# One more step between a chunk's norm and its transposes, and layer 0's last pieces in another order

## The chip, the cores and the metric

The kernel runs on one core of one Trainium2 chip. The metric is the time of one execution on the device, in microseconds (us); lower is better. Times of a kernel are the median of several runs. The profile that is read here comes from one more execution, with the hardware profiler on; its own time stands in the table below.

## What is computed

Two layers work on two images of 128 channels and 64 by 64 points. Layer 0 is a neighbourhood attention block (7 by 7 windows, 4 heads, norms and three linear maps). Layer 1 is a full self-attention over the 4096 tokens of an image, followed by a causal convolution with 16 spectral filters. Cut to what matters for this change:

```python
t = _to_tokens(x)                       # (2, 4096, 128)
t = t + _L1_attn_ref(_ln_t(t))          # softmax(q q^T / sqrt(128), diagonal masked) q
t = t + _L1_ffn_ref(_ln_t(t), ...)      # spectral filters and three short lags
```

The second norm, `_ln_t(t)` after the attention, is the "chunk's norm" of the title. The kernel takes it for 512 tokens at a time, as soon as these 512 tokens have all their attention.

## The kernel before

Layer 0 is written as small pieces (functions named like `t3.pw` or `k.z`), which a table of due times, `PLAN`, sorts. There are 16 bands of 512 tokens, numbered 0 to 15; `t.yr[12]` below is the piece `t.yr` of band 12. Pieces that start with `k` prepare layer 1 for image 0: `k.a` transposes 512 tokens of image 0, `k.tt` copies them, `k.bn` and `k.pw` take the norm's statistics (`k.pw` on POOL), `k.z` applies the norm on POOL in four instructions (L704), `k.b` transposes the normed tokens back on PE (L193), and `k.cm` copies them (L716). Most pieces are issued in a row (`now`, L844). The rest goes into two lists: `chunk_` holds the seven `k` pieces of the last band (15), `later` holds 65 `t` pieces of bands 12 to 15. Before the change they are simply joined (L841). They are issued by `drain` (L1209), three pieces and then a `yield`.

Layer 1's attention (`attention`, L881) treats an image as 8 chunks of 512 tokens and walks over the 36 pairs of chunks `(a, c)` with `a <= c`. For each of the four 128-token tiles of a pair it issues on PE: the scores of the next pair (L898, "weights", one 128x512 product; ACT then takes the exponential, L905), the product with the values (L951 `other`, or L926 `own` where `a == c`), and a product with a turned tile that is left from before (L926 with `et`). After two tiles of a pair with `a != c` come eight 128x128 transposes (L912), whose result DVE copies and sums (L915, tile `et`). After each of the four tiles the code calls `fill()`: this is a slot, into which one step of other work goes.

`filler` (L1189) decides which. It has two queues of generators: `urgent`, for the work that follows a chunk's attention, and `steps`, for work with no hurry (`drain`, the branch weights, the filters' transforms, the tokens of image 1; in the second attention what is left of the first, the mixing of the filter matrices, the loading of blocks). A slot takes one step of `urgent`, and of `steps` only if `urgent` is empty. When row `a` of pairs is finished, `after(b, c, part)` (L968) joins `urgent`. Its steps, with a `yield` after each:

1. PE transposes the chunk's result (L975), DVE divides by the softmax sums and adds the residual (L980).
2. The norm: on DVE `bn_stats` and `bn_aggr` (L174, L175), an add (L164), on POOL a power (L165), on DVE four multiply-subtracts into the tile `z` (L182).
3. PE transposes `z` (L193, four instructions), ACT copies the result into `zc` (L991).
4. and 5. PE multiplies `z` with the transform matrices (L1010), two products each; copies `ub` on DVE and ACT (L1012), stores of `us` by DMA (SP's queue).
6. The last part of the transform (L1020, L1026, L1028).

There are 16 such chunks. After chunks 4 and 8 of an image, `short_lags` (L1034) joins, with transposes of `tt` (L193) and products with `zc` (L1051). At the end of the second attention, the steps that are left of `after` and `short_lags` are issued alternately with those of a `short_lags` that was kept back (`kept`, L1266 to L1271). Then follows the convolution (from L1283), whose inputs `ut` are read back from `us` (L1295).

In the convolution the order on PE is that of the code (`manual_schedule`), and for layer 0's `now` that of all engines. For the slots of the attention a scheduler may still move neighbouring instructions of one engine past each other when the program is built.

Of the kernel before, what the change touches and what calls it, by code (L numbers as in the profile page):

```python
# [95 lines left out]
def kernel(  # L96
# [89 lines left out]
    def layernorm(dst, src):  # L186

        ln_apply(dst, src, ln_statistics(src))

    def transposed(ps, src):  # L190

        for j in range(src.shape[1]):
            nc.tensor.transpose(ps[:, j * P : (j + 1) * P], src[:, j, :], ident)  # L193
# [30 lines left out]
    with l0a:  # L224
# [607 lines left out]
        now, later, chunk_ = [], [], []  # L832
        for at, k, name, f in events:
# [4 lines left out]
            else:  # L838
                early = True
            (chunk_ if name[:1] == "k" and k == bands[-1] else now if early else later).append(f)  # L840
        later = [*chunk_, *later]  # L841
        engines = mybir.EngineType
        with tc.manual_schedule(engines={engines.PE, engines.DVE, engines.Activation, engines.Pool}):
            for f in now:  # L844
# [12 lines left out]
    with ap_:  # L857
# [6 lines left out]
        def bank():  # L864
            return ps_m.tile([P, 512], F32, tag="bank", name="bank")
# [102 lines left out]
        def after(b, c, part):  # L968

            n0 = 4 * c  # L970
            ph, f0 = divmod(n0, FB)
            par, h = divmod(ph, 2)
            pt = bank()
            for j in range(4):
                nc.tensor.transpose(pt[:, j * P : (j + 1) * P], xa[b][:, (n0 + j) * P : (n0 + j + 1) * P], ident)  # L975
            rden = sp.tile([P, 4], F32, tag="rden", name="rden")
            nc.vector.tensor_reduce(rden, part[:, n0 : n0 + 4, :], AX.X, ALU.add)
            nc.vector.reciprocal(rden, rden)
            for j in range(4):
                nc.vector.scalar_tensor_tensor(  # L980
                    tt[b][:, n0 + j, :], pt[:, j * P : (j + 1) * P], rden[:, j : j + 1], tt[b][:, n0 + j, :],
                    ALU.mult, ALU.add,
                )
            yield
            z = sp.tile([P, 4, P], F32, tag="z4", name="z4")
            layernorm(z, tt[b][:, n0 : n0 + 4, :])
            yield
            pt = bank()
            transposed(pt, z)
            s0 = 1 + h * (TH // 2)  # L990
            nc.scalar.copy(  # L991
                zc[:, par, s0 : s0 + TH // 2].rearrange("p (c f) -> p f c", f=FB)[:, f0 : f0 + 4, :],
                pt.rearrange("p (f c) -> p f c", f=4),
            )
            yield
            z2 = z.rearrange("p f d -> p (f d)")

            def store(m0, q, src):
                nc.sync.dma_start(
                    out=us[m0 // 2 : (m0 + P) // 2, :, 2 * h + q, f0 : f0 + 4, b, par, :].rearrange(  # L1000
                        "g r f d -> (g r) f d"
                    ),
                    in_=src.rearrange("p (f d) -> p f d", d=P),
                )

            for m0 in (0, P):
                for q in range(2):
                    rows_ = slice(q * SB, (q + 1) * SB)
                    pu = bank()
                    nc.tensor.matmul(pu, lhsT=tr[rows_, h, m0 : m0 + P], rhs=z2[rows_], start=True, stop=True)  # L1010
                    ub = sp.tile([P, 512], F32, tag="ub", name="ub", bufs=3)
                    (nc.scalar.copy if q else nc.vector.tensor_copy)(ub, pu)  # L1012
                    store(m0, q, ub)
                yield

            banks = [bank() for q in range(2)]
            for i in range(2):
                for q in range(2):
                    rows_ = slice(q * SB, (q + 1) * SB)
                    nc.tensor.matmul(  # L1020
                        banks[q][i * 64 : (i + 1) * 64, 0:256], lhsT=tr[rows_, h, 2 * P : NC],
                        rhs=z2[rows_, i * 256 : (i + 1) * 256], start=True, stop=True,
                    )
            ub = sp.tile([P, 512], F32, tag="ub", name="ub", bufs=3)
            for q in range(2):
                (nc.scalar.copy if q else nc.vector.tensor_copy)(ub[:, q * 256 : (q + 1) * 256], banks[q][:, 0:256])  # L1026
                for i in range(2):
                    nc.sync.dma_start(  # L1028
                        out=us[P:, :, 2 * h + q, f0 + 2 * i : f0 + 2 * i + 2, b, par, :].rearrange("g r f d -> (g r) f d"),
                        in_=ub[i * 64 : (i + 1) * 64, q * 256 : (q + 1) * 256].rearrange("p (f d) -> p f d", d=P),  # L1030
                    )
            yield

        def short_lags(b, h):  # L1034


            for par in range(2):
                n0 = (par * 2 + h) * FB
                for f0 in range(0, FB, 4):
                    pt = bank()  # L1040
                    transposed(pt, tt[b][:, n0 + f0 : n0 + f0 + 4, :])
                    nc.scalar.copy(xa[b][:, (n0 + f0) * P : (n0 + f0 + 4) * P], pt)
                    yield
                xv = xa[b][:, n0 * P : (n0 + FB) * P].rearrange("p (f c) -> p f c", f=FB)
                for c0 in range(0, P, 64):
                    py = bank()
                    for lag in range(3):
                        from_par = (par - lag) % 2
                        back = (lag - par + from_par) // 2
                        s0 = 1 + (h * P + c0) * FB - back  # L1050
                        nc.tensor.matmul(  # L1051
                            py, lhsT=mu[:, lag, :], rhs=zc[:, from_par, s0 : s0 + 512], start=(lag == 0), stop=(lag == 2)
                        )
                    pv = py.rearrange("p (c f) -> p f c", f=FB)
                    first = h == 0 and c0 == 0
                    for lo, hi, s in ((0, 32, 0), (32, 64, 1)) if first else ((0, 64, 2 + h),):
                        xs = xv[:, :, c0 + lo : c0 + hi]
                        nc.vector.scalar_tensor_tensor(
                            xs, pv[:, :, lo:hi], seg[:, s : s + 1], xs, ALU.mult, ALU.add
                        )  # L1060
                    yield
# [127 lines left out]
        def filler(b, steps, kept=None):  # L1189

            urgent, done = [], []

            def fill(c=None, part=None):
                if c is not None:
                    done.append(c)
                    urgent.append(after(b, c, part))
                    if len(done) % 4 == 0:
                        held = kept if kept is not None and len(done) == 4 else urgent
                        held.append(short_lags(b, len(done) // 4 - 1))
                    return  # L1200
                for queue in (urgent, steps):
                    while queue:
                        if next(queue[0], 0) is None:
                            return
                        queue.pop(0)

            return fill, urgent
# [294 lines left out]
```

## Time and profile before

| what | value |
|---|---|
| median of 3 runs | 2224.06 us (2223.95 to 2224.48) |
| the profiled execution's own time | 2225.03 us |
| its span, first to last instruction | 2223.3 us |
| mean granted TensorE clock | 0.992 |
| layer 0 | up to about 346 us of the span |
| attention of image 0 | about 346 to 829 us |
| attention of image 1 and what is left | about 830 to 1319 us |
| convolution | from 1319.4 us |

How to read the lines that follow further down. A list of waits has the engine and line that waited, the engine and line that ended the wait, then the sum in us, the number of times, and the longest. In a timeline each row is a run of like instructions: start, length, engine, line, operation, result and operands, and in brackets the idle time of the engine just before it and what ended it. `x2` behind a 128x512 product is one product[...]. A table by windows gives the busy time of each engine in a stretch, the mean granted TensorE clock (`PEclk`, 1.00 is full) and the share of the DMA engines.

### The profile page before, as it was taken

What the parts mean: (1) busy time and instruction counts of PE and PEld (TensorE: products, weight loads), DVE (VectorE), ACT (ScalarE), POOL (GpSimd) and SP (SyncE); (2) the same over time, 40 slices, a digit from 0 to 9 for tenths busy, and PEclk for the clock granted to TensorE, in tenths of its full rate; (3) what the DMA queues carried; (4) which work ended last, traced back from release to release, by engine and by line L of the source; (5) the groups of instructions that cost most, each with busy time, mean ns of one, the idle gap of its engine ahead of it and who ended that gap; (6) DMA issues with size and microseconds to landing.
All of it is one profiled execution on the core that took longest, in us unless ns stands there. A gap on an engine that the chain in (4) does not pass through costs nothing.

```text
span 2223.3 us, 31764 instructions
## 1 busy us (share of the span) xinstructions
PE 2160.3 (97%) x11920; PEld 1335.6 (60%) x11920; DVE 938.2 (42%) x3054; ACT 778.6 (35%) x1904; POOL 278.1 (13%) x355
## 2 busy tenths in 40 slices
PE   6899998999999999999999999999999999999998
PEld 4677764544544444444544447677677777777776
DVE  5799985334443346433333452222222222222232
ACT  3798883222332223222222332322322222222232
POOL 3477874200000000000000000000000000000000
PEclk9999998999999999999999999999999999999999
DMA  4222212011000015100000132212212121212101
GB/s 147 61 62 61 61 50 52 0 67 52 24 24 24 21 48 164 36 24 24 0 24 24 48 96 54 59 41 58 54 44 59 40 59 40 59 40 59 40 10 76
DMA packets 170344, 110.53 MB, mean 50 GB/s; under 512 B 21311, under 2 KB 155087, under 8 KB 169680
## 3 DMA queue, kind: packets, MB, share of 16 engines
q1 hardware_dynamic: 169266, 105.01, 17.7%
q8 instruction: 94, 1.54, 0.3%
q0 software_dynamic: 576, 2.10, 0.3%
q10 hardware_dynamic: 350, 1.41, 0.2%
q14 instruction: 58, 0.48, 0.1%
HBM read 73.86 MB, written 34.63 MB: 49 GB/s over the span
## 4 chain that ended last, share of the span: by engine, by line
PE 86%; DVE 6%; POOL 4%; DMA 2%; ACT 1%; issue 1%; SPq 1%; POOLq 0%; DVEq 0%; ACTq 0%
PE acc L1326 25%; PE pc L1314 13%; PE bank L898 10%; PE own L926 10%; PE other L951 8%; PE bank L912 4%; PE bank L333 2%; PE bank L193 2%; PE bank L1010 2%; PE bank L1051 1%; PE bank L543 1%; PE py L1348 1%; PE bank L507 1%; ACT p L530 1%; DVE ln_st L379 1%
## 5 line engine op out<-in xcount | busy, mean ns | idle before, releaser
L1315 DVE COPY y<-pc 128x512 f32<-128x512 f32 x320 | 221.4, 692 | 351.6 <-PE pc L1314 347.9
L905 ACT ACTIVATE e<-bank 128x512 f32<-128x512 f32 x288 | 171.8, 597 | 555.1 <-PE bank L898 422.4
L898 PE MATMUL bank<-cm 128*128 128x512 f32 x576 | 298.9, 603 | 1.4 <-DVE y L654 1.4
L1326 PE MATMUL acc<-y,mpl 128*128 128x256 f32 x1280 | 292.1, 382 | 0.0
L1326 PE MATMUL acc<-y,mmi 128*128 128x256 f32 x1280 | 288.0, 379 | 0.0
L1314 PE MATMUL pc<-ct,ut 64*128 64x512 f32 x1280 | 285.2, 595 | 0.9 <-issue 0.9
L1326 PEld LDWEIGHTS acc<-y,mpl 128*128 128x128 f32 x1280 | 238.1, 190 | 59.4 <-issue 29.6
L1326 PEld LDWEIGHTS acc<-y,mmi 128*128 128x128 f32 x1280 | 242.6, 190 | 32.6
L1315 ACT COPY y<-pc 128x512 f32<-128x512 f32 x320 | 204.5, 639 | 87.2 <-PE pc L1314 87.2
L926 PE MATMUL own<-et,tok 128*128 128x512 f32 x448 | 227.3, 594 | 1.7 <-DVE part L915 1.7
L951 PE MATMUL other<-e,tok 128*128 128x512 f32 x448 | 228.6, 592 | 0.0
L1314 PEld LDWEIGHTS pc<-ct,ut 64*128 64x128 f32 x1280 | 121.5, 187 | 145.8 <-issue 140.6
L915 DVE CUSTOM_DVE_ANT_0 et<-bank,one 128x512 f32<-128x512 f32 x224 | 145.6, 687 | 134.4 <-PE bank L912 133.2
L1333 ACT COPY ob<-acc 128x256 f32<-128x256 f32 x32 | 19.0, 594 | 387.0 <-PE acc L1326 387.0
L926 PEld LDWEIGHTS own<-et,tok 128*128 128x128 f32 x448 | 84.3, 190 | 110.5 <-issue 72.3
L951 PEld LDWEIGHTS other<-e,tok 128*128 128x128 f32 x448 | 85.0, 190 | 106.6 <-issue 106.4
L1350 DVE TENSOR_TENSOR xa<-py,xa 128x512 f32<-128x512 f32 x32 | 22.1, 691 | 281.4 <-PE py L1348 281.4
L898 PEld LDWEIGHTS bank<-cm 128*128 128x128 f32 x576 | 95.9, 193 | 73.4 <-issue 43.7
L912 PEld LDWEIGHTS bank<-ident,e 128*128 128x128 f32 x896 | 102.9, 141 | 51.0 <-issue 41.0
L165 POOL TENSOR_TENSOR ln_rs<-ln_rs,mhalf 128x4 f32<-128x4 f32 x24 | 24.3, 1010 | 844.4 <-DVE ln_rs L164 844.4
L530 ACT ACTIVATE p<-p,mn 128x196 f32<-128x196 f32 x256 | 114.4, 449 | 12.9 <-DVE mn L520 12.3
L912 PE MATMUL bank<-ident,e 128*128 128x128 f32 x896 | 117.2, 274 | 0.0
(210 smaller groups left out, 2292.8 us busy)
## 6 DMA issues: line engine op xcount, KB each, us to landing
ut<-us SPq DMA_DIRECT2D x80, 256.0 KB
us<-ub SPq DMA_DIRECT2D x64, 256.0 KB
vw<-vd SPq DMA_DIRECT2D x256, 49.0 KB
ct<-gs SPq DMA_DIRECT2D x160, 72.0 KB
ct<-gs SPq DMA_DIRECT2D x160, 64.0 KB
gs<-sum SPq DMA_DIRECT2D x20, 256.0 KB
vd<-v SPq DMA_DIRECT2D x128, 32.0 KB
st<-in_m_plus_dram SPq DMA_DIRECT2D x16, 256.0 KB
```

Of the source, the lines that this page charges most:

```text
L193: nc.tensor.transpose(ps[:, j * P : (j + 1) * P], src[:, j, :], ident)
L333: nc.tensor.matmul(pl, lhsT=wg[:, lo : lo + P], rhs=zT, start=True, stop=True)
L530: nc.scalar.activation(p, p, AF.Exp, bias=t[name + "mn"][:, h : h + 1], scale=-1.0, accum_out=t["den"][:, u, h : h + 1],)
L898: nc.tensor.matmul(ps, lhsT=cm[b][:, n * P : (n + 1) * P], rhs=cm[b][:, chunk(c)], start=True, stop=True)
L905: nc.scalar.activation(e, ps, AF.Exp, bias=0.0, scale=ASCALE, accum_out=part[:, n, c : c + 1])
L912: nc.tensor.transpose(pt[:, k * P : (k + 1) * P], es[k][:, m * P : (m + 1) * P], ident)
L915: nc.vector.tensor_tensor_reduce(et, pt, one, 1.0, 0.0, ALU.mult, ALU.add, part[:, n, a : a + 1])
L926: nc.tensor.matmul(own, lhsT=tok[b][:, n, :], rhs=e, start=first, stop=last)
L951: nc.tensor.matmul(other, lhsT=tok[b][:, 4 * CHUNKS[a] + j, :], rhs=es[j], start=(j == 0), stop=(j == 3))
L1314: nc.tensor.matmul(pc, lhsT=ut[fp, b, par, :], rhs=cv_[fp], start=True, stop=True)
L1315: (nc.scalar.copy if f else nc.vector.tensor_copy)(y[:, 4 * f : 4 * f + 4, :, par, b * 2 * FB + q : (b + 1) * 2 * FB : 2], pc.rearrange("p ...
L1326: nc.tensor.matmul(acc, lhsT=(mmi if l else mpl)[:, k, :], rhs=y[:, 1::2, k, ::-1, :] if l else y[:, 0::2, k, :, :], start=(l == 0 and k = ...
```

## The change

Three edits. `after` gets a step that issues nothing, between the norm and its transposes; it yields `True`. `fill` learns what that means: at `None` the slot is used up as before, at `True` the queue is left as it is and the next queue gets its turn in the same slot, and a generator that has ended (`False`) is dropped. So in that one slot a step of `steps` is issued, if there is one, and otherwise nothing. And `later` is joined in another order.

```diff
-        later = [*chunk_, *later]
+
+        later = [*chunk_[:3], later[2], *chunk_[3:5], *later[:2], *later[3:5], *chunk_[5:], *later[5:]]
...
             z = sp.tile([P, 4, P], F32, tag="z4", name="z4")
             layernorm(z, tt[b][:, n0 : n0 + 4, :])
             yield
+            yield True
             pt = bank()
             transposed(pt, z)
...
+
                 for queue in (urgent, steps):
                     while queue:
-                        if next(queue[0], 0) is None:
+                        got = next(queue[0], False)
+                        if got is None:
                             return
+                        if got:
+                            break
                         queue.pop(0)
```

The first slots of `drain`, by the names of the pieces:

```
before: k.a, k.tt, k.bn | k.pw, k.z, k.b | k.cm, t.proj[15], t.pb[15] | t.yr[12], t.add[12], t3.bn[12] | t3.pw[12], ...
after:  k.a, k.tt, k.bn | t.yr[12], k.pw, k.z | t.proj[15], t.pb[15], t.add[12] | t3.bn[12], k.b, k.cm | t3.pw[12], ...
```

From `t3.pw[12]` on both lists are the same. At the end of the second attention (L1268 to L1269) every `yield` of `after`, the new one too, also draws a step of `kept`.

## The prediction

> **What bounds the kernel now.** I read the page first (busy shares), then PE's list of waits, then the timelines of PE and DVE around each wait, last the table by windows for the clock.
>
> ```profile
> PE 2160.3 (97%) x11920; PEld 1335.6 (60%) x11920; DVE 938.2 (42%) x3054; ACT 778.6 (35%) x1904; POOL 278.1 (13%) x355
> ```
> PE is the bound: it is idle for 2223.3 - 2160.3 = 63 us, and nothing else is near full. A change that only moves work can win PE's idle time and PE's time at a low clock, no more. PE's waits:
>
> ```profile
> PE bank L193 <- DVE z L182: 15.1, 14, 3.8
> ...
> PE bank L193 <- POOL tok L704: 6.3, 10, 2.6
> ```
> The first row is what the new step aims at: 14 of the 16 chunks' transposes wait for `z`. The timeline of PE shows them one by one: 0.67 us once, 0.74 us ten times, then 1.60 (at 827.8), 3.83 (849.3) and 1.60 (1284.7). A typical one, PE and below it DVE:
>
> ```profile
> 464.33 1.02 PE L898 MATMUL bank<-cm 128*128 128x512 f32 x2
> 465.19 1.02 PE L926 MATMUL own<-e,tok 128*128 128x512 f32 x2
> 466.05 1.02 PE L898 MATMUL bank<-cm 128*128 128x512 f32 x2
> 466.90 1.02 PE L926 MATMUL own<-e,tok 128*128 128x512 f32 x2
> 468.60 0.75 PE L193 MATMUL bank<-ident,z 128*128 128x128 f32 x3 [0.67 <-DVE z L182]
> ```
> ```profile
> 468.11 1.11 DVE L182 TENSOR_SCALAR z<-tt,ln_mv,ln_rs 128x128 f32<-128x128 f32 x4 [1.12 <-POOL ln_rs L165]
> ```
> Starts are 0.86 us apart: that is a product's price here (the 1.02 overlaps). PE is ready at 467.93, `z` is whole at 469.22. The other place is the last `k.b`:
>
> ```profile
> 357.44 0.47 PE L193 MATMUL bank<-ident,tok 128*128 128x128 f32 x1 [2.63 <-POOL tok L704]
> 358.63 0.47 PE L193 MATMUL bank<-ident,tok 128*128 128x128 f32 x1 [0.72 <-POOL tok L704]
> 359.41 0.47 PE L193 MATMUL bank<-ident,tok 128*128 128x128 f32 x1 [0.30 <-POOL tok L704]
> 360.18 0.47 PE L193 MATMUL bank<-ident,tok 128*128 128x128 f32 x1 [0.30 <-POOL tok L704]
> 360.45 1.92 PE L898 MATMUL bank<-cm 128*128 128x512 f32 x2
> 362.16 1.92 PE L602 MATMUL bank<-w_sb,att 128*128 128x128 f32 x8
> ```
> 3.95 us of waiting for POOL's four L704 (3.54 us from 356.59). Then L898 and L602 are 1.71 us apart, twice 0.86. The windows say why (second number: length; after the engines: PEclk):
>
> ```profile
> 355.00:360.00 5.00, 1.42 (x3) 0.54 (x3) 1.52 (x9) 0.00 (x0) 4.80 (x7) 0.75 1.19 99
> 360.00:365.00 5.00, 4.82 (x14) 3.24 (x15) 2.12 (x7) 2.04 (x5) 1.37 (x3) 0.57 0.25 71
> ```
> PE's clock was halved from about 357.5 to 364.3, after the idle time. The same stands behind the other long waits: 0.76 in 850 to 855, 0.66 in 1285 to 1290.
>
> [...] half rate followed 2.63, 3.83 and 1.60 us of idling, but not the 1.60 us at 827.8[...]. [...] (at 844.9 us L980 starts 3.9 us after its transposes, behind sums of filter matrices that waited for DMAs). So a wait can go from `z` to whatever stands behind `z` on DVE.
>
> **The change part by part.** No instruction is added or taken away; the step is empty. What moves I took from the order of instructions in the built programs, both of them.
>
> Typical chunks (11 waits, 0.67 + 10 x 0.74 = 8.1 us). One more L898 and L926 now stand before the transposes of `z`: 2 x 0.86 = 1.72 us of cover. PE comes at 467.93 + 1.72 = 469.65, 0.43 us after all of `z`. The wait goes. What is late next: on DVE two `ub` copies and two `et` follow `z`, and PE needs the first `et` after the eight L912 and two products, 2.6 us after L1010; copy and `et` take 0.7 + 0.7 us with at most 0.2 us of start each. Covered. Banks: the new order puts L951 before the second L1010 and L912 before L1020; as before, three separate groups of 64-row products remain, each with its 1.06 us step. In the first attention a step of `steps` also slips in (two filter products, or the transposes of `tok`); it was to be issued anyway, a few slots later. The step's stores are one slot later on SP's queue, which has nothing before the end that waits for them. Gain 8.1, bounds 7 and 8.5.
>
> The last `k.b`. POOL's order is unchanged, so L704 stays where it is, and so does the first wait's end. On PE two L898, one L926 and `t.proj` (L602, 0.87 us), 3.4 us, go ahead of the transposes. PE arrives at about 358.2, finds two tiles ready, waits some 0.5 us for the others and is done near 360.6, as before, but with 3.4 us of work behind it that used to follow, most of it at half clock. If the halving goes with the wait, PE is at the first L912 at 364.0 instead of 369.23: 5.2 us. Then DVE is late: its chain of `t.pb` (about 363), statistics, POOL's power (1.3 us), L416 stands ahead of the first `et`, which I work out for 367.6; PE wants it at 366.6. That gives back 1.0. ACT has a risk of the same sort: the third exponential now stands behind L407 (end 362.5), needed at 364. Net 4.2; bounds 1.5 (halving stays, more waiting) and 5.5.
>
> End of the first attention (827.8): one transpose still comes directly after the last L926, so the 1.60 us stay. Start of the second (849.3, 3.83 us): the transposes of `z` now come after eight L912, L898, L951 and an L926 with `et`. But in DVE's order that `et` stands behind `z`, and five small filter instructions have slipped ahead of L980. I get the `et` 9.65 us after L975 against 6.05 us of work on PE: a wait of 3.6 us with another name. Gain 0.2, half clock after it as now; bounds -1.5 and +3.
>
> After the second attention: the 1.60 us at 1284.7 stay (nothing is put in between). The following four L1010, 3.53 us at half clock, are now parted by transposes of `tt`. For the last chunk, PE works 3.4 us after L975 (three L1051, eight L193) before it wants `z`; in DVE's order two L1058 and then a third stand inside the norm, so `z` comes about 5.4 us after L975: a new wait of 2.0 us, where six L1051 covered it before. Part of it comes back in the L1010 (up to 1.4 us). The convolution's first product waits for `ut`, whose load is issued when the second of three late groups of L193 is done (1313.4) and takes 6.0 us, 0.89 us longer than the six L1051 that cover it. These last steps are in the same order; the stores of the last part come nearer, about 0.6 + 5.3 = 5.9 us after L1020, and the L193 6.9 us after it: still PE. Loss 0.6; bounds a gain of 1.5 and a loss of 4.
>
> Sum: 8.1 + 4.2 + 0.2 - 0.6 = 11.9 us. The profiled execution took 2225.03 us (span 2223.3 and 1.7 around it), so 2213.1 there; the median shown is 0.97 lower: 2212.1.
>
> **Rivals.** All against the median.
>
> A: the first part wins, the last `k.b` gives nothing (DVE and ACT take over, clock still halved) and the tail loses 3: 8.1 + 0 + 0.2 - 3 = 5.3, time 2218.8. For it: the L613 and `et` chain; against it: DVE has only 1.52 of 5 us busy there.
>
> B: more than the forecast: no halving near 849 and 1286 any more (about 1.6 us each), 3.0 us in all [...]: 2209. For it: 827.8 went without halving. Against it: both waits remain.
>
> C: slower. The wait passes from `z` to `et`, because [...] the stolen step puts statistics of image 1's tokens ahead of `et`: about 2.5 us of DVE and 1.1 us of waiting for POOL, against a margin of about 1.0 us. Price 2.6 us at a chunk; only the first attention has such steps, at most 6 chunks, 15.6 us. Won stay the second attention's 6 x 0.74 = 4.4 and 3.8 from the other parts: 2224.1 + 15.6 - 8.2 = 2231.5. It decides from 1.4 us a chunk on, that is 2.4 us of extra DVE time. Against it: in the built order of DVE only one sum (0.7 us) stands there, at one chunk.
>
> D: no change: PE's modelled ends hide waits that are no loss, and 8.1 us of idle were slack; only 3.8 are won. Time 2220.3. Against it: PE is 97% busy and everything behind is in order.
>
> **How the numbers follow.** Forecast 70%, A 12, B 11, C 3, D 4. The likeliest: 2212. The range of 2208 to 2218 takes in the bounds of the four terms, B and most of A; some 15% are left out. A measurement of this kernel tells a change of about 0.2%, 4.4 us, from none: below 2219.6 counts as faster, 0.92; within, D and the rest of A, 0.05; slower, 0.03.
>
> **What would show it.** The row of L193 waiting for `z` falls from 15.1 us in 14 to about 5 in 3 or 4; the one for `tok` loses its longest; PEclk between 355 and 365 is near 1.00; a new row of about 4 us, L926 waiting for `part` (L915), appears at the start of the second attention. I am wrong if L926 waits for `et` at most chunks, or if the halved clock comes back elsewhere.

## The result and the profile after

| | before | after |
|---|---|---|
| median (range, runs) | 2224.27 us (2223.95 to 2224.59, 4) | 2209.86 us (2207.72 to 2211.93, 4) |
| profiled execution | 2225.03 us | 2211.93 us |
| its span | 2223.3 us | 2210.2 us |
| mean granted TensorE clock | 0.992 | 0.992 |

The ratio is 0.9935, with a 95% interval of 0.9918 to 0.9952: 14.4 us faster. The forecast was 2212 us for the median (2212.1 by its sum) and 2213.1 us for the profiled execution. The code after the change stands one or two lines lower (L898 is now L899, L915 is L916, L926 is L927, L951 is L952, L975 is L976, L980 is L981, L1010 is L1012, the `ub` copies of L1012 are L1014, L1051 is L1053, L1058 is L1060, L1117 is L1119); in some of the experiments it stands a few lines lower still.

First the busy shares from the page of after, and under them the first rows of its list of TensorE's waits (sum, times, longest, in us):

```profile
PE 2156.2 (98%) x11920; PEld 1335.0 (60%) x11920; DVE 938.0 (42%) x3054; ACT 780.6 (35%) x1904; POOL 278.5 (13%) x355
```
```profile
PE bank L349 <- DVE gmv L344: 10.6, 1, 10.6
PE own L927 <- DVE part L916: 7.4, 6, 4.4
PE bank L193 <- DVE z L182: 5.1, 3, 1.9
...
PE bank L193 <- POOL tok L704: 3.1, 8, 0.5
```

The row for `z` fell from 15.1 us in 14 waits to 5.1 in 3. The row of L927 waiting for `part`, 4.4 us at its longest, stands among the longest now. The row for `tok` lost its longest wait. The idle time is 2210.2 - 2156.2 = 54 us, where it was 63.

A typical chunk, TensorE's timeline of after:

```profile
464.37 1.12 PE L899 MATMUL bank<-cm 128*128 128x512 f32 x2
465.33 1.02 PE L927 MATMUL own<-e,tok 128*128 128x512 f32 x2
466.19 0.60 PE L193 MATMUL bank<-ident,z 128*128 128x128 f32 x4
466.63 1.02 PE L899 MATMUL bank<-cm 128*128 128x512 f32 x2
```

There is no bracket, and the four transposes take 0.44 us from start to start. The last `k.b` and what follows:

```profile
358.28 0.41 PE L193 MATMUL bank<-ident,tok 128*128 128x128 f32 x2
359.19 0.33 PE L193 MATMUL bank<-ident,tok 128*128 128x128 f32 x1 [0.49 <-POOL tok L704]
359.96 0.33 PE L193 MATMUL bank<-ident,tok 128*128 128x128 f32 x1 [0.45 <-POOL tok L704]
360.13 1.02 PE L899 MATMUL bank<-cm 128*128 128x512 f32 x2
...
367.14 1.12 PE L927 MATMUL own<-et,tok 128*128 128x512 f32 x2 [0.82 <-DVE part L916]
```

TensorE comes at 358.28, finds two tiles ready, waits 0.94 us for the other two, and later 0.82 us for `et`. The windows there (after the engines: granted clock, DMA share, GB/s) show that the clock stayed full:

```profile
355.00:360.00 5.00, 4.06 (x18) 2.12 (x17) 1.79 (x12) 0.69 (x2) 4.64 (x7) 1.00 1.34 88
360.00:365.00 5.00, 5.00 (x19) 2.80 (x20) 3.02 (x14) 1.92 (x5) 1.65 (x4) 1.00 0.33 95
```

The start of the second attention did not go as well. TensorE and, below it, VectorE:

```profile
830.88 0.60 PE L976 MATMUL bank<-ident,xa 128*128 128x128 f32 x4
...
841.93 2.07 PE L927 MATMUL own<-et,tok 128*128 128x512 f32 x2 [4.42 <-DVE part L916]
843.79 1.06 PE L193 MATMUL bank<-ident,z 128*128 128x128 f32 x4
844.65 1.91 PE L899 MATMUL bank<-cm 128*128 128x512 f32 x2
846.35 1.78 PE L952 MATMUL other<-e,tok 128*128 128x512 f32 x2
847.97 1.02 PE L927 MATMUL own<-et,tok 128*128 128x512 f32 x2
```
```profile
831.77 1.60 DVE L1119 SCALAR_TENSOR_TENSOR mmi<-st,wt,mmi 128x512 f32<-128x512 f32 x2 [3.23 <-DMA st<-in_m_minus_dram]
...
836.05 1.12 DVE L981 SCALAR_TENSOR_TENSOR tt<-bank,rden,tt 128x128 f32<-128x128 f32 x4
...
840.15 1.11 DVE L182 TENSOR_SCALAR z<-tt,ln_mv,ln_rs 128x128 f32<-128x128 f32 x4 [0.90 <-POOL ln_rs L165]
841.18 0.68 DVE L916 CUSTOM_DVE_ANT_0 et<-bank,one 128x512 f32<-128x512 f32 x1
```

The transposes of `xa` end at about 831.5, but VectorE starts L981 only at 836.05: it had stood 3.23 us, up to 831.77, before a filter sum whose load had not landed, and then worked through this sum, a second one and eight more instructions, seven of them for the filters. `et` follows `z` and comes at 841.8. From 841.93 to 847.97 TensorE takes 6.04 us for what costs 0.86 + 0.44 + 0.86 + 0.86 = 3.02 at full clock: about 3.0 us lost to a halved clock, which lasts from 841.1 to 847.9.

To sum up by stages I took the start of each chunk's transposes of `xa` (L975, after L976) in both traces; the time from one to the next is a row of pairs of chunks. Gains in us, profiled execution against profiled execution:

| stage | predicted | measured |
|---|---|---|
| layer 0 up to the attention, same code | 0 | -0.16 |
| last `k.b` (attention's start to chunk 0: 117.49, then 112.78) | 4.2 | 4.71 |
| typical chunks, first attention (six rows, 0.62 to 1.25 each) | 8.1 with the next line | 6.45 |
| typical chunks, second attention (six rows, 1.16 to 1.17 each) | see above | 6.99 |
| end of the first and start of the second attention (129.93, then 132.70) | 0.2 | -2.77 |
| last chunk up to the convolution, with the row before it (39.48, then 41.60) | -0.6 | -2.12 |
| sum | 11.9 | 13.10 |

The sum is the difference of the spans. The total was close because two errors of opposite sign met: the typical chunks gave 5.3 us more than predicted, the two ends 4.5 us less.

### The profile page after: what moved, and what is told of

It is laid out like the page before. It is cut to its first block, busy times and chain, and to the rows that moved or that the text cites. A ratio compares the mean times of both kernels' runs of the same rounds, so it can differ in the third digit from the quotient of the medians.

```text
span 2210.2 us, 31763 instructions
## 1 busy us (share of the span) xinstructions
PE 2156.2 (98%) x11920; PEld 1335.0 (60%) x11920; DVE 938.0 (42%) x3054; ACT 780.6 (35%) x1904; POOL 278.5 (13%) x355
## 4 chain that ended last, share of the span: by engine, by line
PE 88%; DVE 5%; POOL 3%; DMA 2%; ACT 1%; issue 1%; SPq 1%; POOLq 0%; DVEq 0%; ACTq 0%
PE acc L1332 25%; PE pc L1320 13%; PE own L927 11%; PE bank L899 11%; PE other L952 8%; PE bank L913 4%; PE bank L333 2%; PE bank L1053 2%; PE bank L193 1%; PE bank L543 1%; PE bank L1012 1%; PE py L1354 1%; PE bank L507 1%; DMA st<-in_m_minus_dram 1%; PE po L565 1%; DVE ln_st L379 1%
## 5 line engine op out<-in xcount | busy, mean ns | idle before, releaser
L899 PE MATMUL bank<-cm 128*128 128x512 f32 x576 | 297.9, 601 | 1.4 <-DVE y L654 1.4
L927 PE MATMUL own<-et,tok 128*128 128x512 f32 x448 | 228.5, 597 | 7.5 <-DVE part L916 7.4
L952 PE MATMUL other<-e,tok 128*128 128x512 f32 x448 | 229.7, 594 | 0.0
L916 DVE CUSTOM_DVE_ANT_0 et<-bank,one 128x512 f32<-128x512 f32 x224 | 145.5, 687 | 131.5 <-PE bank L913 131.4
L927 PEld LDWEIGHTS own<-et,tok 128*128 128x128 f32 x448 | 84.4, 191 | 117.5 <-issue 73.3
L952 PEld LDWEIGHTS other<-e,tok 128*128 128x128 f32 x448 | 85.2, 191 | 107.8 <-issue 106.0
L899 PEld LDWEIGHTS bank<-cm 128*128 128x128 f32 x576 | 94.5, 191 | 67.9 <-issue 44.7
```

The costliest lines, as they stand in the source:

```text
L899: nc.tensor.matmul(ps, lhsT=cm[b][:, n * P : (n + 1) * P], rhs=cm[b][:, chunk(c)], start=True, stop=True)
L916: nc.vector.tensor_tensor_reduce(et, pt, one, 1.0, 0.0, ALU.mult, ALU.add, part[:, n, a : a + 1])
L927: nc.tensor.matmul(own, lhsT=tok[b][:, n, :], rhs=e, start=first, stop=last)
L952: nc.tensor.matmul(other, lhsT=tok[b][:, 4 * CHUNKS[a] + j, :], rhs=es[j], start=(j == 0), stop=(j == 3))
```

## Experiments

### The two parts apart: e1, e2, e3

e1 has the new step alone (`later` as before), e2 the new order alone (without the step and with the old `fill`), e3 the new order, and the step only for image 1.

```diff
e1  -        later = [*chunk_[:3], later[2], *chunk_[3:5], *later[:2], *later[3:5], *chunk_[5:], *later[5:]]
e1  +        later = [*chunk_, *later]
e2  -            yield True
e3  -            yield True
e3  +            if b == 1:
e3  +                yield True
```

> The new step alone, with layer 0's pieces in the old order. Theory S: a covered wait is worth the start-to-start time that PE lost, about 1.17 us at a chunk (0.91 us until the first transpose and 0.26 us because the transposes follow DVE's pace), not the 0.74 us of the bracket; with the loss at the start of the second attention (2.8) and behind it (2.1) that leaves about 8.5 us: 2215 to 2216. The wait of 3.95 us before 360 us and the halved clock behind it are back, PEclk about 0.57 between 360 and 365. Theory G: a wait is worth its bracket, 0.74, and the rest of the gain came with the reordered pieces: about 4 us, 2220.

> The new order of layer 0's last pieces alone, without the new step. Theory S: 4.7 us, 2219.6; the first transposes of image 0's first chunk come 4.5 us earlier, PEclk is 1.00 between 355 and 365, and from there on all distances are those of the kernel before (14 waits for z, 15.1 us). Rival: the reordered pieces also feed the later stages, and the gain grows to 8 or more between 370 and 830 us.

> Both edits, but the new step only for image 1's chunks. Theory S: 4.7 from the order, 7.0 from six chunks of the second attention (1.17 each), a loss of about 2 behind it, and the start of the second attention as in the kernel before (a wait of 3.8 for z, no wait of L927 for et there): 9.6 us, 2214.7. Theory G (0.74 a chunk): 7.0 us, 2217.3. If the loss of 2.8 us at the start of the second attention does not come from image 0's last chunks, it shows here too and the time is 2217 or more.

| run | median (range, runs) | ratio to before (95%) |
|---|---|---|
| e1, step only | 2212.85 (2211.68 to 2214.61, 5) | 0.9944 (0.9932 to 0.9957) |
| e2, order only | 2219.94 (2218.45 to 2224.30, 20) | 0.9980 (0.9973 to 0.9986) |
| e3, step for image 1, new order | 2214.18 (2212.24 to 2215.95, 5) | 0.9949 (0.9937 to 0.9962) |

Before was 2224.75 us beside them (2222.40 to 2227.51, 24 runs). By stages, in us:

| stage | before | after | e1 | e2 | e3 |
|---|---|---|---|---|---|
| attention's start to chunk 0 | 117.49 | 112.78 | 117.84 | 112.73 | 113.03 |
| chunk 0 to 1 | 100.38 | 99.28 | 99.28 | 100.38 | 100.38 |
| chunk 11 to 12 | 48.51 | 47.35 | 47.35 | 48.51 | 47.35 |
| chunk 6 to 8 (between the attentions) | 129.93 | 132.70 | 132.91 | 131.92 | 130.66 |
| last chunk to the convolution, with the row before it | 39.48 | 41.60 | 40.00 | 39.35 | 41.53 |

At the last `k.b` and at the typical chunks the parts add up. The order alone brings the 4.7 us at the last `k.b` and at most 0.1 us at a typical chunk; the step alone brings 1.1 to 1.25 us at every typical chunk (0.62 at chunk 2) and nothing at `k.b`; in e3 only image 1's chunks gain. The medians do not quite add up: e1 gains 11.9 us and e2 4.8, both together 14.4. A rule by which the idle time at `z` was slack is excluded: e1 is 12 us faster than before. The row between the attentions disagrees: it is 2.0 us longer in e2 and 0.7 us longer in e3, where image 0's chunks have no new step. In e2 TensorE waits 4.45 us for `z` there, and the 4.80 us behind it bring 2.46 us of work, about half rate; in e3 it waits 1.60 us (at 819.9) and 2.27 us (at 841.4), and behind them 1.7 and 1.6 us are lost at half rate (L1013 takes 2.00 us to the next start at 820.84, L899 1.85 at 842.32).

In e1 the clock is halved at the last `k.b` again, where TensorE waits 2.44, 0.45, 0.69 and 0.30 us for `tok`:

```profile
355.00:360.00 5.00, 3.82 (x10) 2.31 (x11) 1.82 (x7) 2.04 (x5) 3.17 (x5) 0.57 0.53 72
360.00:365.00 5.00, 5.00 (x13) 2.54 (x12) 2.52 (x12) 1.23 (x4) 1.26 (x2) 0.75 0.19 52
```

So S held against G: a chunk is worth more than the 0.74 us in its bracket. The time of e1 still came out 2 us below what S had given: the loss behind the second attention, expected as 2.1 us, was 0.52, since no halved clock followed the wait there, and layer 0, whose code is the same, was 2.8 us shorter than before in the profiled execution. Chunk 0 shows where the price beyond the bracket comes from. Before, TensorE's timeline goes on like this behind the lines of the prediction:

```profile
469.19 1.02 PE L898 MATMUL bank<-cm 128*128 128x512 f32 x2
470.05 0.27 PE L193 MATMUL bank<-ident,z 128*128 128x128 f32 x1
470.16 1.02 PE L926 MATMUL own<-e,tok 128*128 128x512 f32 x2
```

The L926 before it starts at 466.90, and the next instruction could start 0.86 us later, at 467.76. The first transpose starts at 468.60: 0.84 us lost, not 0.67, because the bracket counts from the modelled end of the bar (466.90 + 1.02), 0.17 us after that point. Then the transposes follow VectorE's pace: 0.59 + 0.11 = 0.70 us of TensorE instead of the 0.44 seen in after, 0.26 more. 0.84 + 0.26 = 1.10, and the row is shorter by 1.10. For brackets of 0.74 us it comes to 0.91 + 0.26 = 1.17.

### Is the length of the wait at `k.b` what counts: e5

After, with the last `k.b` only one slot behind `k.z`, so that it comes earlier by some work.

```diff
-        later = [*chunk_[:3], later[2], *chunk_[3:5], *later[:2], *later[3:5], *chunk_[5:], *later[5:]]
+        later = [*chunk_[:3], later[2], *chunk_[3:5], *chunk_[5:], later[0], later[1], *later[3:]]
```

> The changed kernel, but the last k.b comes one slot after k.z, not two, so that PE meets POOL's four instructions about 1.7 us before the first is done. Theory W: the halved clock follows from a long wait; this one is shorter than before (some 1.7 us and three times 0.45), the clock stays at 1.00 between 355 and 365 us, and the first L913 comes 2.6 us later after the attention's start than in the changed kernel, of which the wait for et behind it gives back 0.8. About 1.7 us slower than the changed kernel. Theory C: any wait there halves the clock (PEclk 0.5 to 0.8 behind it): 3.5 us or more slower.

2212.04 us (2210.63 to 2212.62, 4 runs; before 2224.61), ratio 0.9941 (0.9926 to 0.9956), which can't be told from after by the time. The stage tells: from the attention's start to chunk 0 it takes 117.01 us, 4.2 more than in after and nearly the 117.49 of before. TensorE's timeline:

```profile
355.30 0.33 PE L193 MATMUL bank<-ident,tok 128*128 128x128 f32 x1 [1.53 <-POOL tok L704]
356.18 0.33 PE L193 MATMUL bank<-ident,tok 128*128 128x128 f32 x1 [0.56 <-POOL tok L704]
357.00 0.48 PE L193 MATMUL bank<-ident,tok 128*128 128x128 f32 x1 [0.49 <-POOL tok L704]
357.77 0.48 PE L193 MATMUL bank<-ident,tok 128*128 128x128 f32 x1 [0.30 <-POOL tok L704]
358.04 1.92 PE L602 MATMUL bank<-w_sb,att 128*128 128x128 f32 x8
```

TensorE waits 2.88 us in four pieces, and the clock is halved from 356.8 on, within the third of them (L602 takes 1.71 us to the next start, 0.89 in after). So a wait that is 1.07 us shorter than before brought only 0.5 us: W, by which it would leave the clock full, fell. Of C the halving came. Its time did not: by the medians e5 is 2.2 us slower than after, not 3.5, and that is within the noise. Nor does any wait halve the clock: after has waits of 0.49, 0.45 and 0.82 us there at full clock. Here the profiled execution loses less in the sum than in this stage because layer 0, whose code is the same, was 2.1 us shorter in it, and its last chunk ran at full clock.

### More distance: e4 and e8

`yield True` twice (e4) and three times (e8).

```diff
             yield True
+            yield True
```

> Both edits, with two empty steps instead of one. Theory S: the typical chunks were fully covered and win nothing (distances between chunks unchanged within 0.1 us); only the waits that one step left can win: the 1.6 us before the second attention, and the 4.4 us for et with its halved clock at its start, since et now stands ahead of z on DVE: 2202 to 2207. Rival: each further step pushes the rest of a chunk's work to where it collides (the end of a row, the stores before the convolution), and the time rises to 2211 to 2214.

> Three empty steps. Theory S: nothing is left to cover at typical chunks, so their distances stay; what two steps left (1.5 us at the end of the second attention, 2.5 at its start) may go: 2199 to 2202. Rival: a chunk's work now runs past the end of its row and into the tail: slower than with two steps, 2204 or more.

e4 took 2202.43 us (2201.66 to 2203.46, 4 runs), ratio 0.9897 (0.9883 to 0.9910). From the first list of e4's waits:

```profile
PE own L927 <- DVE part L916: 5.5, 7, 2.5
...
PE bank L193 <- DVE z L182: 1.5, 1, 1.5
```

Against after the profile gains 4.9 us between the attentions (127.77 us) and 4.5 us at the last chunk (37.13 us), and no more than 0.05 us at each typical chunk, which had no wait left. Between the attentions the longest wait is 2.5 us, and no halved clock follows it (L899, L952 and L927 start 0.86 us apart from 839.33 on); the last chunk's `z` is ready when TensorE wants it.

The third step took back part of what the second gave: 2205.85 us (2204.09 to 2207.37, 4 runs), ratio 0.9916 (0.9900 to 0.9933).

The rows from chunk 2 to chunk 6 are 2.4 us longer than in e4, with a wait of 1.23 us for image 1's tokens that e4 does not have:

```profile
640.15 1.10 PE L193 MATMUL bank<-ident,tok 128*128 128x128 f32 x4 [1.23 <-DVE tok L182]
```

Between the attentions it takes 129.34 us, 1.6 more than in e4, and about 1.8 us are lost at half rate there (L899 and L952 take 1.75 and 1.71 us to the next start at 835.61 and 837.36). I take it that more steps of `steps` are drawn early, before what they wait for is ready; no run tests this, and the other 1.2 us of the 2.4 I did not trace to a wait. The time is the one that the rival had forecast, but not at its place: the last chunk up to the convolution takes 36.80 us, no longer than in e4.

### Who is late at the start of the second attention: e6, e7, e9

The prediction had blamed VectorE's order: small filter instructions ahead of L980. e6 lets the filter sums (`mixed` in `filter_matrices`) depend on the normed tokens of image 0's last chunk, by adding 0 times a piece of `zc` to their weights `wt`, so that they can't stand ahead of that chunk's norm in VectorE's queue; e7 is e4 with the same line. e9 is e7 with the same done to the scaling of `inv` (four small instructions that wait for another load), which then depends on image 1's normed tokens (the new tile `seg_` is left out of the diff).

```diff
e6   def filter_matrices(mpl, mmi):
e6  +    nc.vector.scalar_tensor_tensor(wt, zc[:, 1, 1029:1033], 0.0, wt, ALU.mult, ALU.add)
e9  +    nc.vector.scalar_tensor_tensor(seg_, zc[:, 1, 1029:1033], 0.0, seg, ALU.mult, ALU.add)
e9       for s, (lo, hi) in enumerate(((0, 32), (32, 64), (64, 128), (128, 256))):
e9  -        nc.vector.tensor_scalar(inv[:, :, lo:hi], inv[:, :, lo:hi], seg[:, s : s + 1], None, ALU.mult)
e9  +        nc.vector.tensor_scalar(inv[:, :, lo:hi], inv[:, :, lo:hi], seg_[:, s : s + 1], None, ALU.mult)
```

> The changed kernel, but the mixing of the filter matrices depends on the transposes of image 0's last chunk (its weights are rewritten by one small instruction that reads zc), so that none of it can stand ahead of that chunk's norm on DVE. Theory D: the wait of 4.4 us for et at the start of the second attention is DVE's backlog of filter work that itself waited for DMAs; it falls under 0.5 us, the halved clock behind it goes, and the second attention's start (from image 0's seventh chunk to image 1's first) takes 125 to 127 us in place of 132.7: 2203 to 2204. Rival: the wait is the norm's own chain (DVE, POOL, DVE) ahead of et; it stays above 3 us and the time within 2 us of the changed kernel's.

> Two empty steps, and the filter matrices held back as in the run before. Theory D: the waits of 2.5 and 1.0 us at the start of the second attention go as well: 3 us below the kernel with two steps, 2199. Rival: held back, the filter work meets the short lags' and the next chunk's DVE work and costs as much there: 2202 to 2204.

> Built on e7_two_filters_late; the only further edit makes the scaling of inv (four small VectorE instructions that wait for a load) depend on image 1's normed tokens, so that it can't stand ahead of the last ub copies of image 0. D (what is left at the start of the second attention is the same mechanism, VectorE standing in order behind a load: in the profile of e7 it waits 6.56 us for inv's load and TensorE then 1.64 us for ub): rows 7 and 8 together fall by 1.6 us, from 125.5 to about 123.9, the wait of 1.64 us is gone, time 2197.2 (2196.5 to 2197.9). Rival (TensorE is held there by something else, or the wait moves to another load): rows 7 and 8 within 0.5 of 125.5, time 2198.3 to 2199.3.

| run | median (range, runs) | ratio to before (95%) | chunk 6 to 8 |
|---|---|---|---|
| after | 2209.86 (2207.72 to 2211.93, 4) | 0.9935 (0.9918 to 0.9952) | 132.70 |
| e6 | 2203.82 (2202.45 to 2204.79, 4) | 0.9904 (0.9890 to 0.9919) | 126.99 |
| e7 | 2198.79 (2198.00 to 2198.96, 4) | 0.9882 (0.9867 to 0.9896) | 125.49 |
| e9 | 2197.31 (2196.80 to 2198.16, 4) | 0.9869 (0.9852 to 0.9885) | 124.11 |

VectorE in e6 at that place:

```profile
831.33 1.12 DVE L981 SCALAR_TENSOR_TENSOR tt<-bank,rden,tt 128x128 f32<-128x128 f32 x4
...
835.99 0.69 DVE L916 CUSTOM_DVE_ANT_0 et<-bank,one 128x512 f32<-128x512 f32 x1
...
839.72 0.16 DVE L1123 SCALAR_TENSOR_TENSOR wt<-zc,wt 128x4 f32<-128x4 f32 x1 [2.42 <-ACT zc L993]
```

The filters' sums start behind L1123, `et` is there in time, and TensorE waits for neither `et` nor `z` at that place (one wait of 1.08 us for a `ub` copy is left). The granted clock is 1.00 throughout from 835 to 855 us, where in after it is 0.60 from 840 to 845 and 0.71 from 845 to 850. The row shrank by 5.7 us, where the wait of 4.42 and the halved clock of 3.0 had stood. So the prediction's cause was right: `et` stood in VectorE's order behind the filter work. e6 moves all of that work away, and so it doesn't part the time that VectorE stood before loads from the time that the sums themselves take.

In e7 what is left of it is the wait for the load of `inv`:

```profile
829.55 1.11 DVE L1290 TENSOR_SCALAR inv<-inv,seg 128x96 f32<-128x96 f32 x4 [6.56 <-DMA inv<-t_out]
830.58 0.68 DVE L1015 COPY ub<-bank 128x512 f32<-128x512 f32 x1
```
```profile
831.31 0.66 PE L976 MATMUL bank<-ident,xa 128*128 128x128 f32 x4 [1.64 <-DVE ub L1015]
```

e9 removes that wait and brings 1.4 us in the row; 0.81 us of waiting for a `ub` copy on ScalarE take its place. Its time fell as expected, though its interval and that of e7 overlap. e9 has the lowest time of all versions: 0.9869 of before, where after has 0.9935.

### The last chunk: e10

e6, but at the end of the second attention the new yield draws no step of `kept`.

```diff
-            for _ in gen:
-                next(kept, None)
+            for got in gen:
+                if got is None:
+                    next(kept, None)
```

> Built on e6_filters_late; at the end of the second attention the new yield no longer draws a step of the kept short_lags. V (the prediction's account: the last chunk's z is late because two products' updates stand inside its norm on VectorE, and that order is unchanged): the wait for z in the last chunk stays at 1.9 to 2.3 us, and from the last chunk's transposes of xa to the convolution it takes 27.7 to 28.2 us (27.72 in e6). K (the extra draw is what brings z's transposes too early): the wait is below 0.5 us and the stretch is 26.0 to 26.5 us. One look: the profile decides, the time differs by less than 2 us (V 2203 to 2205, K 2201 to 2203).

A single run: 2206.00 us (e6 2203.82). From the last chunk's L976 to the convolution it takes 30.02 us, where e6 has 27.72:

```profile
1270.81 2.74 PE L1053 MATMUL bank<-zc,mu 128*128 128x512 f32 x6
1273.39 0.60 PE L193 MATMUL bank<-ident,tt 128*128 128x128 f32 x4
1276.38 0.30 PE L193 MATMUL bank<-ident,z 128*128 128x128 f32 x1 [2.39 <-DVE z L182]
...
1277.59 2.08 PE L1012 MATMUL bank<-z,tr 64*128 64x512 f32 x4
```

The wait for `z` did not go, it grew from 1.86 to 2.39 us, because the drawn step (four transposes of `tt`) had covered part of it. So the extra draw is not what makes `z` late, and K fell. The prediction's account, products' updates (L1060) that VectorE has ahead of and inside the norm, is read from VectorE's order and not tested by an edit: in after L981 to L182 takes 4.45 us at 1279.66, with an update of 0.75 us between them, and 3.63 us in e6 at 831.33 with none. The wait was a little over the range expected, and half rate followed it (L1012 takes 2.01 us to the next start instead of 1.06, the L1053 behind it 3.20 instead of 2.77); the two made the stretch 2.3 us longer than in e6.

## Why the prediction was right, and where it was not

- Typical chunks (predicted 8.1, bounds 7 and 8.5; measured 13.4): the wait went at all of them, as said, and no other took its place; the step is the right one and its size was wrong. The failing term is "11 waits, 0.67 + 10 x 0.74 = 8.1 us": it took the bracket for the whole price. Start to start, a chunk lost 1.10 to 1.25 us (of the 1.25 at chunk 1, 0.09 came in e2 without the step), and chunk 2, whose transposes had no bracket at all before, gained 0.62 us: there they came 0.21 us late and took 0.85 us for 0.44, which no list of waits shows. The starts needed for this were in the trace of before.
- The last `k.b` (4.2; measured 4.71, and 4.76 with the order alone): right in size and in cause. The 1.0 us taken off for a late `et` was there as a wait of 0.82 us. Of the gain 2.2 us are waiting (5.33 us in all in this stage before, 3.14 after); the other 2.5 us I put down to the clock. In e5, with the halved clock back, 1.1 of the 4.2 us lost are waiting and 3.1 the rest. The halving began at 357.5 before the change, after one wait of 2.63 us, and at 356.8 in e5, after waits of 1.53 and 0.56 us and a part of 0.49.
- End of the first attention (the 1.60 us wait stays): right, it is 1.59 us at 816.81.
- Start of the second attention (gain 0.2, bounds -1.5 and +3; measured -2.77): right in what becomes late, `et` behind VectorE's queue, and roughly in the size of the wait (3.6 predicted, 4.42 measured). Two terms failed. The `et` was to come 9.65 us after the transposes of `xa`; it came 11.0 us after them, as VectorE started L981 5.2 us behind them (4.3 before). And "half clock after it as now": it lasted 6.8 us instead of 3.4. Before:

```profile
849.25 1.16 PE L193 MATMUL bank<-ident,z 128*128 128x128 f32 x4 [3.83 <-DVE z L182]
850.20 1.92 PE L898 MATMUL bank<-cm 128*128 128x512 f32 x2
852.04 1.28 PE L1010 MATMUL bank<-z,tr 64*128 64x512 f32 x4
853.26 1.09 PE L912 MATMUL bank<-ident,e 128*128 128x128 f32 x8
```

  There the halved clock cost 0.95 + 1.84 + 1.22 us for work of 0.44 + 0.96 + 1.06, 1.5 us; after the new wait about 3.0. With 0.6 us more of the wait this makes 2.1 of the 2.8; 0.6 us are two later waits for `et` (0.55 and 0.85 us, 0.63 and 0.20 before). But the length of the halved clock does not decide the loss. In e1 and e5 a wait of the same size (4.41 and 4.27 us) was followed by only about 3.4 us of it (1.7 us lost in each), and the row between the attentions is as long (132.91 and 132.77 us): the two later waits for `et` are longer there, in e1 1.44 and 1.15 us. How much the step costs here stays open: without it the row takes 129.93 us (before), 130.66 (e3) and 131.93 (e2), with it 132.70 to 132.91.
- After the second attention (loss 0.6; measured 2.12): the new wait of 2.0 us for the last chunk's `z` is there with 1.86 us (at 1284.51). What failed is "Part of it comes back in the L1010 (up to 1.4 us)": the four L1010 were parted by transposes of `tt`, but the halved clock then slowed those as well. In after:

```profile
1269.51 1.01 PE L193 MATMUL bank<-ident,z 128*128 128x128 f32 x4 [1.60 <-DVE z L182]
1270.44 1.45 PE L1012 MATMUL bank<-z,tr 64*128 64x512 f32 x4
1271.82 1.11 PE L193 MATMUL bank<-ident,tt 128*128 128x128 f32 x4
1272.86 1.94 PE L1012 MATMUL bank<-z,tr 64*128 64x512 f32 x4
1274.74 0.66 PE L193 MATMUL bank<-ident,tt 128*128 128x128 f32 x4
```

  From 1270.44 to 1274.74 the two groups of L1012 and the transposes between them take 4.30 us for 2.70 us of work, 1.6 us lost, as much as before the change (3.53 us for 1.93). In e1, e5 and e6, which have the same waits and where this halving did not occur, the stretch is 1.6 us shorter (40.00 us in each).
- Rivals: A (the order gives nothing) is excluded by e2; C (the wait passes to `et` at every chunk) by the rows of 1.1 to 1.2 us; D (the idle time was slack) by e1. B had forecast nearly the time that came, 2209, but for a reason that did not occur: the halving near both ends is still there in after, at 841.1 and 1271.1.

What the prediction named as signs came as well: the row for `z` at about 5 us, a longest wait of about 4 us for `part`, a clock of 1.00 between 355 and 365. Its sign for being wrong, a halved clock that comes back elsewhere, came in part, 3.4 us longer at 841.1.

So the forecast of the time was close, the reasons for the sign were right, and the closeness of the size was partly luck: +5.3 us at the typical chunks against -3.0 and -1.5 us at the two ends.

## What to carry to other kernels

Price a wait by the starts before and behind it, not by its bracket alone: here 0.74 us in the list were 1.17 us in the row, and 0.26 of the difference came from transposes that ran at VectorE's pace once TensorE had caught up with it. Before moving work into or out of a bracket, look at what stands ahead of the producer on its own engine: here filter sums that waited for loads (3.23 us up to 831.77 in after) held up L981 and the norm behind them, and making them depend on something later (e6) was worth 6 us beside the 14 of the whole change. Where a wait is followed by a halved clock, a somewhat shorter wait may win next to nothing: at the last `k.b` 2.88 us in place of 3.95 won 0.5 us (e5), and 0.94 us, after which the clock stayed full, won 4.7.

## What was not expected of the hardware

- The halved stretches of before and after last 3.4 or 6.8 us by the clock records of their traces (10.2 and 13.7 us near 40 us; the last one ends with the kernel). In after the four that begin at 315.4, 335.9, 841.1 and 1271.1 are 20.48, 505.17 and 430.08 us apart, which is 6, 148 and 126 times 3.413 us, the length of a short one. Which wait is followed by a halved clock stays open: 1.60 us of waiting for `z` was at 1269.5 in after and was not at the same instructions in e1, e5 and e6; 1.86 us at 1284.5 in after was not, and 2.39 us in e10 was.
- Layer 0, with the same code in all versions, reached the attention at 346.4 us in before, 346.6 in after, 344.5 in e5 and 344.4 in e8. Its late halved stretches fell differently: in before one of 6.8 us from 333.6, in after two of 3.4 us from 315.4 and 335.9. A difference of 2 us between two profiled executions is thus not yet a difference of the kernels; the lengths of the typical chunks' rows, equal within 0.25 us for equal code and mostly within 0.02, told more than the total times.
